# Two pairs projected before the first attention step, and constant products on TensorE, in a gated attention block

## The chip, the cores and the metric

The kernel runs on one NeuronCore of one Trainium2 chip. The metric is the time of one execution in device microseconds. Five engines work side by side, each through its own instructions in their order: TensorE (PE, with its weight loads shown as PEld), VectorE (DVE), ScalarE (ACT), GpSimd (POOL), and SyncE (SP), which here only issues DMAs. Semaphores let one engine wait for another.

## What is computed

One block of a gated cross-attention network, for 4 batches of 512 tokens, width 512. The tokens are normalized twice and rounded to fp8 with a scale for each input. From them come the queries, keys and values of a self-attention (8 groups, 2 heads each, depth 128) and the queries of a cross-attention whose keys and values come from a second sequence. Queries and keys are normalized over their depth. Then a projection and a feed-forward part with ternary weights follow.

```python
ln_out = _ln(hidden_states, ln_w, ln_b)
q = _fp8_linear_pertensor(ln_out, wq, wq_scale, q_in_scale).reshape(b, s, g, hpg, d)
q = _ln(q, qln_w, qln_b)
k = _fp8_linear_pertensor(ln_out, wk, wk_scale, k_in_scale).reshape(b, s, g, d)
k = _ln(k, kln_w, kln_b)
v = _fp8_linear_pertensor(ln_out, wv, wv_scale, v_in_scale).reshape(b, s, g, d)
core = _gqa(q, k, v).reshape(b, s, nh * d)
...
cat = jnp.concatenate([core, xout], axis=-1)
catq = _div_clamp_fp8(cat, proj_smooth)
return jnp.einsum('bsi,oi->bso', catq, wproj) * (proj_in_scale * proj_w_scale)
```

## The kernel before

A *block* is one group of one batch: its queries, keys and values. It is made in two *pairs* (`Pair`, L503), each of two tiles of 128 tokens, so pair k belongs to block k // 2. The order of the blocks is a string in `PLAN` ("ord", two digits for group and batch): the first are group 0, 1 and 2 of batch 0, then groups 1, 0, 2 and 3 of batch 1. Pairs 0 and 1 need the weights of group 0, pairs 2 and 3 those of group 1, pairs 4 and 5 those of group 2, and pair 6 is the first that needs batch 1.

A tile of a pair passes through these steps. `mm` (L519) is 24 products of PE into a PSUM tile of its own (ps_p, one buffer for each half). `sq` (L544) squares queries and keys on ACT (jk), `vals` copies the values (vv), `var` (L554) makes the factors (DVE and POOL, ss). `out` (L571) scales the queries on ACT (z) and then the keys on DVE (y, yj, z), which frees the PSUM tile. When both tiles are out, `split` (L588) writes high and low parts (hl, on ACT and POOL), and `turn` transposes them by DMA into qk.

A *unit* (`Unit`, L604) is one head of one block. For each half of its tokens: `scores` (PE, 8 products into ps_s), `top` (their maxima, mx, DVE), `top_turn` (two transposes, mt, PE), `shift` (nm, DVE) and a DMA of nm into qk, `shift_mm` (4 products that subtract the maximum), `exps` (pt, ACT), `pv` (po, PE, 16 products as the trace counts them) and `evac` and `quant` (r and ob, DVE).

`step(s, k)` (L826) is one unit s with one pair k, in two halves. In each half the scores of the new half unit come first, then the tile that was projected two halves ago is put out, the last one gets its squares, the older half units go on, and `q.mm((h,))` projects a tile of pair k. So a projection waits until the tile two halves back has left its buffer. With s = -1 a step has no new unit, only a pair. The loop at L1173 runs the steps; `extra` says before which of them a step without a unit is put. Before the loop, the head (from L939 on) prepares batch 0, the weights of groups 0 and 1, and projects pairs 0, 1 and 2 by hand.

Work for later pairs lies in `behind`: the rest of batch 1, the weights of group 2 and 3 (`weights_2`, `weights_3`), batches 2 and 3. Each weight chunk (four a group) has a mean and shift (ms), scalings of three 128-column parts (wf), a high part (ACT) and a low part (DVE, wq). `ws` says which engine scales each part: v is DVE, s is ACT. Each batch chunk has four transposes on PE (ps_t), four scalings on ACT (yb) and three operations on DVE (yb, yb, xa). `beside` (L914) hands out pieces in each half against a budget for DVE and ACT (`bg`, and `bg0` where there is no new unit). `at_hook` (L907) puts a batch chunk's transposes inside a projection. `need` (L931) finishes what a pair needs before it starts. `w2` is how many pieces of group 2's weights the head takes, in two places.

The order on each engine is the order of the program while `Ordered.on[0]` is set, for all engines but SP's loads through `sy`. All recorded operations share one line of the code, so the profile shows L75 for them and the tile names tell them apart.

Of the kernel before, what the change touches and what calls it, by code (L numbers as in the profile page):

```python
# [9 lines left out]
F32 = mybir.dt.float32  # L10
# [9 lines left out]
B, S, H = 4, 512, 512  # L20
# [29 lines left out]
    "gain": [66, 69, 74, 77, 82, 85, 90, 93, 98, 101],  # L50
    "ch": [104, 105, 106, *range(108, 116), *range(117, 125)],
    "wp16": 68,
    "extra": {2: 1, 6: 1},
    "none": [],
    "bs": "ssss",
    "w2": [0, 5],
    "ws": "vvs",
    "bg": [1.5, 2.7],
    "bg0": [3.0, 3.0],
}  # L60

# [22 lines left out]
def flamingo_kernel(  # L84
# [18 lines left out]
    cfg = PLAN  # L103
    v, sc, pe, gp, so = [Ordered(tc, e) for e in (nc.vector, nc.scalar, nc.tensor, nc.gpsimd, nc.sync)]
# [11 lines left out]
    ident = const.tile([128, 128], F32, name="ident")  # L116
    make_identity(nc, ident)
    ones = const.tile([128, 128], F32, name="ones")
# [16 lines left out]
    pp_o = keep.enter_context(tc.tile_pool(name="pp_o", bufs=1, space=PSUM))  # L135
# [105 lines left out]
    def consts_out(load_rsr):  # L241
        v.reciprocal(rsm, smo)

        v.tensor_scalar(
            rsm[:, 0:16], rsm[:, 0:16], cs[:, 2:3], 2.0**-8, ALU.mult, ALU.mult
        )
        v.tensor_scalar(
            rsm[:, 16:32], rsm[:, 16:32], 2.0**-8 / KVX_SCALE, None, ALU.mult
        )

        rt = pp_o.tile([128, S], F32, name="rt", tag="po", bufs=1)
        pe.transpose(rt[0:NCH, 0:128], rsm, ident)
        rr = const.tile([NCH, 128], F32, name="rr")
        v.tensor_copy(rr, rt[0:NCH, 0:128])
        so.dma_start(out=rsm_d, in_=rr)
        for i in range(2):
            load_rsr(i)
# [25 lines left out]
    with attn as ph:  # L283
# [25 lines left out]
        def load_rsr(i):  # L309

            rsr[i] = cp.tile([128, 8, 128], F32, name="rsr", bufs=2)
            so.dma_start(
                out=rsr[i].rearrange("p c d -> p (c d)"),
                in_=rsm_d[8 * i : 8 * i + 8].rearrange("c (o d) -> o (c d)", o=1).broadcast_to((128, 1024)),
            )
# [615 lines left out]
        def need(k):  # L931

            blk = pair_block(k)
            for item in list(behind):
                if item[0] in ((blk.ty, blk.g), blk.b):
                    while advance(item) is not None:
                        pass

        Ordered.on[0] = True  # L939
        b0, w0 = Batch(0), Weights(0, 0, wf0)  # L940
        first = consts_first()
# [35 lines left out]
        def scale0(ic, on, ts=range(3)):  # L977
            b0.ps = pss[ic]
            b0.scale(ic, on, ts)
# [36 lines left out]
                b0.fp8(ic, 2)  # L1016
        for p in pairs:
            p.mm((0, 1), (NIC - 1,))
        for ic in range(NIC):
            scale0(ic, "s", (3,))  # L1020
            b0.store(ic)
# [58 lines left out]
        ]  # L1080
        b1.factor()
        consts_out(load_rsr)
        w2 = behind[1]
        for _ in range(cfg["w2"][0]):
            advance(w2)
# [80 lines left out]
        def proj2_mm(ps, t, chunks=range(NCH)):  # L1166
            for c in chunks:
                pe.matmul(
                    ps, cats[t][:, c], wp[c // 12][:, c % 12], start=(c == 0), stop=(c == NCH - 1)
                )  # L1170

        now = 3
        for s in range(n_steps):  # L1173
            Ordered.on[0] = s < n_steps - 3
            if s in (36, 68):
                load_rsr(s // 32 + 1)
            for _ in range(cfg["extra"].get(s, 0)):
                step(-1, now)
                now += 1
            if s in cfg["none"]:  # L1180
                step(s, None)
            else:
                step(s, now)
                now += 1
            to_go = n_steps - s
            if to_go == 4:
                early.update({i: pp_p.tile([128, 512], F32, name="ps_p", tag=f"pp{i}") for i in range(2)})
            for i, chunks in cfg["early"].get(str(to_go), ()):
                proj2_mm(early[i], i, range(*chunks))
# [257 lines left out]
```

## Time and profile before

| What | Value |
|---|---|
| median of 3 runs | 1730.95 us (1727.8 to 1731.91) |
| profiled execution | 1728.55 us |
| its span, first to last instruction | 1726.8 us |
| PE busy | 1639.6 us, 95% |
| DVE busy | 1280.2 us, 74% |
| ACT busy | 1075.1 us, 62% |
| POOL busy | 564.3 us, 33% |

The page of the profile has a row for each engine over 40 equal slices of the span, some 43 us each, in which a digit is the busy share in tenths; the row PEclk is the granted clock of PE in tenths of full speed. Other views answer for a stretch of time: what an engine waited for, its instructions in order of time, or busy times by stretches.

In the first slices PE is busy about half of the time or less, from the fourth on nearly always. Up to about 23 us the clock row says full speed, but 12 products there take 1.89 us (at 18.65) and 1.05 us at 23.66.

### The profile page before, as it was taken

How to read it: one execution, taken by the hardware profiler on the slowest of the kernel's cores; microseconds unless marked ns; L12 is line 12 of the kernel's file. 1: busy time of each engine (PE TensorE's matmuls, PEld its weight loads, DVE VectorE, ACT ScalarE, POOL GpSimd, SP SyncE). 2: the span in 40 equal slices, each digit the busy share in tenths (PEclk: the TensorE clock that was granted, in tenths of full speed). 3: DMA queues.
4: the chain of work that ended last, by engine and by line, in shares of the span. 5: the costliest groups of instructions: out<-in, count | busy, mean ns of one | idle time of the engine just before them, and what ended most of it. 6: DMA issues, size and time to landing. Idle time of an engine off the chain costs nothing.

```text
span 1726.8 us, 40358 instructions
## 1 busy us (share of the span) xinstructions
PE 1639.6 (95%) x14662; PEld 1394.2 (81%) x14662; DVE 1280.2 (74%) x3849; ACT 1075.1 (62%) x3270; POOL 564.3 (33%) x740
## 2 busy tenths in 40 slices
PE   4578999999999998999999999999999999999999
PEld 3468899999999997889999999999999976444444
DVE  8677777777777778877777777777666665679786
ACT  7667676666666666666666666666665543457443
POOL 2223334333334336543444443433333320110000
PEclk8789999999999999999999999999999999999999
DMA  5334445444544556545677676764545684974434
GB/s 166 73 76 82 86 78 96 87 85 87 102 89 87 87 110 137 133 77 114 123 117 123 117 123 117 119 118 93 93 105 111 117 184 151 285 244 110 86 78 87
DMA packets 495144, 196.56 MB, mean 114 GB/s; under 512 B 455232, under 2 KB 463456, under 8 KB 493280
## 3 DMA queue, kind: packets, MB, share of 16 engines
q1 hardware_dynamic: 403888, 139.43, 40.7%
q10 hardware_dynamic: 86448, 50.36, 12.1%
q0 software_dynamic: 4608, 4.20, 1.9%
q8 instruction: 114, 1.87, 0.4%
q14 instruction: 86, 0.70, 0.1%
HBM read 88.90 MB, written 27.28 MB: 67 GB/s over the span
## 4 chain that ended last, share of the span: by engine, by line
PE 77%; DVE 5%; ACT 3%; DMA 3%; issue 2%; POOL 1%; SPq 0%; ACTq 0%
PE ps_p L75 25%; PE po L75 21%; PE ps_s L75 16%; PE psj L75 5%; PE psd L75 3%; PE ub L75 3%; PE ga L75 3%; DMA qk<-nm 2%; PE mt L75 1%; DVE mx L75 1%; ACT yb L75 1%; DVE xa L75 1%; ACT xa L75 1%; DVE nm L75 1%; DVE ob L75 1%
## 5 line engine op out<-in xcount | busy, mean ns | idle before, releaser
L75 PE MATMUL ps_p<-wq,xa 128*128 128x256 f16 (+1 forms) x5584 | 554.2, 256 | 26.9 <-ACT jk L75 13.1
L75 DVE TENSOR_REDUCE mx<-ps_s 128x256 f16<-128x1024 f32 x256 | 334.2, 1305 | 304.9 <-PE ps_s L75 304.9
L75 PEld LDWEIGHTS <-xa 128*128 128x128 f16 x5632 | 480.6, 99 | 77.5 <-issue 15.6
L75 ACT ACTIVATE pt<-ps_s 128x1024 f32<-128x1024 f32 x256 | 262.7, 1026 | 427.0 <-PE ps_s L75 394.7
L75 PE MATMUL po<-vv,pt 128*128 128x129 f32 x4096 | 500.8, 276 | 1.7 <-ACT pt L75 1.7
L75 PEld LDWEIGHTS po<-vv,pt 128*128 128x128 f32 x4096 | 479.1, 192 | 5.1 <-ACT pt L75 2.0
L75 POOL TENSOR_TENSOR ss<-ss,mhalf 128x3 f32<-128x3 f32 (+1 forms) x254 | 220.5, 868 | 738.3 <-DVE ss L75 555.4
L75 PE MATMUL ps_s<-qk 128*128 128x256 f16 x3072 | 421.4, 274 | 9.5 <-DMA qk<-nm 4.2
L75 PEld LDWEIGHTS <-qk 128*128 128x128 f16 x3072 | 286.1, 98 | 40.8 <-issue 9.5
L75 POOL TENSOR_TENSOR hl<-z,hl 128x768 f16<-128x768 f32 x126 | 207.7, 1648 | 94.3 <-ACT hl L75 94.3
L75 ACT ACTIVATE jk<-ps_p 128x128 f32<-128x128 f32 x762 | 201.6, 284 | 10.0 <-PE ps_p L75 8.8
L75 ACT ACTIVATION_READ_ACCUMULATOR jk<-ps_p 128x1 f32 x762 | 164.8, 216 | 0.0
L75 DVE SCALAR_TENSOR_TENSOR ob<-po,r,rsr 128x128 bf16<-128x128 f32 x512 | 156.0, 347 | 8.8
L75 ACT ACTIVATE z<-ps_p,ss 128x127 f32<-128x127 f32 x508 | 156.4, 360 | 7.4 <-issue 3.6
L75 ACT CAST hl<-z 128x768 f16<-128x768 f32 x128 | 106.5, 832 | 28.8 <-POOL z L75 28.8
L75 DVE TENSOR_SCALAR ob<-ob 128x512 bf16<-128x512 bf16 (+2 forms) x384 | 112.1, 292 | 8.8
L75 DVE TENSOR_REDUCE nm<-mt 128x2 f16<-128x256 f16 x256 | 107.0, 418 | 2.0 <-PE mt L75 2.0
L75 PEld LDWEIGHTS <-nt 128*128 128x128 bf16 x512 | 50.0, 98 | 63.6 <-issue 4.3
L75 DVE SCALAR_TENSOR_TENSOR y<-ps_p,ss,gk 128x128 f32<-128x128 f32 x254 | 87.0, 342 | 14.8 <-ACT z L75 9.4
L75 PEld LDWEIGHTS <-cat 128*128 128x128 f16 x512 | 50.0, 98 | 59.1 <-DMA cat<-cat_d 0.9
L75 PE MATMUL mt<-ident,mx 128*128 128x128 f16 x512 | 70.8, 220 | 27.9 <-DVE mx L75 27.9
L75 PE MATMUL psj<-wp,cat 128*128 128x512 f16 x448 | 96.9, 379 | 0.0
(144 smaller groups left out, 1591.3 us busy)
## 6 DMA issues: line engine op xcount, KB each, us to landing
cat_d<-ot ACTq DMA_DIRECT2D x128, 128.0 KB, 2.9
wf<-in_dram ACTq DMA_DIRECT2D x52, 256.0 KB, 3.6
cat<-cat_d SPq DMA_DIRECT2D x13, 1024.0 KB, 5.6
wt<-in_dram ACTq DMA_DIRECT2D x48, 256.0 KB, 4.5
wt<-in_dram SPq DMA_DIRECT2D x24, 512.0 KB, 4.0
xt<-in_dram SPq DMA_DIRECT2D x32, 256.0 KB, 4.0
qk<-nm SPq DMA_DIRECT2D x256, 0.5 KB, 2.0
cf<-in_dram SPq DMA_DIRECT2D x16, 256.0 KB, 2.9
```

What stands on the lines that cost most here:

```text
L75: ins = f(*args, **kw)
```

## The change

Three things are changed, all by the plan and by a helper of four lines.

First, `extra` was one step without a unit before step 2 and one before step 6. Now two such steps stand before step 0. So pairs 3 and 4 are projected before the first scores, and step s is run with pair s + 5 from the start.

Second, `keep_busy(n)` makes n products of `ident` and `ones` into a PSUM tile with the tag "rb", which the transposes ps_t and mt also use, and nobody reads it. It is called with 26 after the last products of pairs 0 and 1, with 32 after `consts_out` (the transpose rt), and with 10 between the two steps without a unit.

Third, `w2` goes from 0 and 5 pieces to 1 and 8, `ws` gives the third scaling of each chunk of groups 2 and 3 to DVE, and `bg` changes a little.

```diff
-    "extra": {2: 1, 6: 1},
+    "extra": {0: 2},
     "none": [],
     "bs": "ssss",
-    "w2": [0, 5],
-    "ws": "vvs",
-    "bg": [1.5, 2.7],
+    "w2": [1, 8],
+    "kb": [26, 32, 10],
+    "ws": "vvv",
+    "bg": [1.4, 2.8],
...
+        def keep_busy(n):
+
+            t_ = pp_o.tile([128, S], F32, name="kb", tag="rb", bufs=1)
+            for _ in range(n):
+                pe.matmul(t_[:, 0:128], ident, ones, start=True, stop=True)
+
...
         for p in pairs:
             p.mm((0, 1), (NIC - 1,))
+        keep_busy(cfg["kb"][0])
...
         consts_out(load_rsr)
+        keep_busy(cfg["kb"][1])
...
-            for _ in range(cfg["extra"].get(s, 0)):
+            for i in range(cfg["extra"].get(s, 0)):
                 step(-1, now)
                 now += 1
+                if s == 0 and i == 0:
+                    keep_busy(cfg["kb"][2])
```

## The prediction

> **What bounds the kernel now.** I began with the busy shares by slice, then took two stretches of the span.
>
> ```profile
> span 1726.8 us, 40358 instructions
> PE   4578999999999998999999999999999999999999
> PEclk8789999999999999999999999999999999999999
> 46.70:160.00 113.30, 80.24 (x764) 71.20 (x765) 75.71 (x220) 76.87 (x228) 31.92 (x40) 0.88 0.33 73
> 160.00:1700.00 1540.00, 1515.25 (x13634) 1295.78 (x13632) 1150.98 (x3474) 959.54 (x2950) 521.14 (x673) 1.00 0.57 116
> ```
>
> The first number after a stretch's length is PE's busy time, the first after the brackets its granted clock. After 160 us PE idles 25 us in 1540: PE is the bound, and the change leaves its instructions there as they were. From 46.7 to 160 us PE idles 33 us of 113 at a mean clock of 0.88. The change works here, so I asked what PE waited for from 28 to 160 us, and read PE's order of time (the first: total, times, longest; the second: start, duration, and in brackets PE's idle time before).
>
> ```profile
> PE mt L75 <- DVE mx L75: 16.0, 7, 5.4
> PE ps_p L75 <- ACT jk L75: 11.2, 6, 3.4
> PE ps_s L75 <- DMA qk<-hl: 2.8, 1, 2.8
> ```
>
> ```profile
> 46.82 1.52 PE L75 MATMUL ps_s<-qk 128*128 128x256 f16 x8
> 53.76 0.39 PE L75 MATMUL mt<-ident,mx 128*128 128x128 f16 x2 [5.43 <-DVE mx L75]
> 54.30 3.43 PE L75 MATMUL ps_p<-wq,xa 128*128 128x256 f16 x24 [0.15 <-DVE yj L75]
> ...
> 83.35 1.94 PE L75 MATMUL ps_p<-wq,xa 128*128 128x256 f16 x24 [3.23 <-ACT jk L75]
> 88.68 3.32 PE L75 MATMUL ps_p<-wq,xa 128*128 128x256 f16 x24 [3.39 <-ACT jk L75]
> ...
> 101.64 0.28 PE L75 MATMUL mt<-ident,mx 128*128 128x128 f16 x2 [1.51 <-DVE mx L75]
> ...
> 126.20 1.04 PE L75 MATMUL ps_s<-qk 128*128 128x256 f16 x4 [2.82 <-DMA qk<-hl]
> ...
> 159.82 0.28 PE L75 MATMUL mt<-ident,mx 128*128 128x128 f16 x2
> ```
>
> The same 24 multiplications (one half of a pair) take 1.94 us at full clock and 3.43 or 3.32 at half. The first scores run at 46.8, but their maxima (mx, DVE) come only at 53.7, since DVE is in the weights of group 2. Pair 5, projected without a unit beside it, has its halves at 83.35 and 88.68: 5.3 us for 1.77 of work. The wait on qk<-hl at 126.2 is pair 5, projected at 83 to 92 and needed by step 4: too small a lead.
>
> **The change, part by part.** Milestones: A is mt of step 1, first half, after the rest of batch 1; B is mt of step 6, first half. From B on both programs have the same order on PE but for a few transposes. Before, B is at 159.82.
>
> *The 26 constants.* PE idles from 28.51 to 37.05. An f32 product of this size costs 0.11 us at full clock (po: 16 in 1.95, less 0.17 for the last to end), so 2.9 us, ending near 31.4. Cover: that pause; at half clock 5.7, still covered. Gain: none. What follows pair 2 is rsm on DVE at 46.64, and DVE's own chain (four statistics after the low parts) sets that, not PE. Without the cover they would cost 2.9.
>
> *The 32 constants* start when rt is done, about 47.0; at half clock 0.22 each, until the clock comes on, so they end between 50.5 and 54. What PE does next is pair 3, first half, which needs pair 2 out of PSUM: statistics, ACT z, then DVE y and yj. That chain now has two weight chunks ahead of it instead of one and a half: DVE's third scaling (0.85 for x3 against 0.60 for x2), one more mean (0.55), shift (0.2) and low (0.62), while ACT saves two scalings of 0.48. Following ACT: norms from 48.1 to 50.95, chunk 0 high 51.8, chunk 1 high (after DVE's scaling, 53.4) 54.0, tanh, z 54.7; then y and yj to 55.4. So pair 3 starts at 55.45, 1.15 later than before, and the constants fit under it. Uncovered they would cost 3.5 to 7. Their worth is that pair 3's halves take 1.77 instead of 3.4, about 2 us of what reaches the next chain.
>
> *Pairs 3 and 4 ahead of step 0.* By the same FIFO walk (jk 0.25 a piece, vv 0.29, yb 2.8, hl 0.8, wf swv 0.3, high 0.53, POOL ss 0.85, z 0.62, y with yj 0.6): pair 3's second half starts at 58.55 (z at 57.8); its transposes let yb run from 60.05 to 62.8; chunk 3's high ends at 63.6, z at 64.15, so pair 4 starts at 64.95. Its second half starts at 67.9 if DVE is not held by POOL's hl and at 70.4 if it is; I take 69. *The 10 constants* wait for yb, since they share the bank of the transposes: 62.85 to 63.95, before 64.95. Cover one us; without it 1.1. Doubled, at half clock, they would delay pair 4 by 0.1.
>
> *Step 0.* PE ends pair 4 at 71.2, scores 72.1, mx 74.0, pair 5 at 74.6, second scores 77.3, pair 5's second half about 79.8 to 81.6. Then the rest of batch 1: before, its first transpose was at 91.84 and mt at 101.64, of which 1 us was half clock; here 81.6 + 9.4 gives A at 91.0. Bounds: 89.5 without a hold, 93 with every hold and cold transposes.
>
> *Steps 1 to 5* are ten halves. Before, the eight halves from 101.64 to 149.95 took 6.04 each. The wait of 2.82 on qk<-hl goes, with about 0.8 of half clock behind it: pair 5 is now projected four units ahead. That gives 5.59. Some of what DVE and ACT caught up in that pause comes back, so I take 5.9: ten halves 59, B at 150.0. Bounds: 5.0 a half is PE's own work (scores 0.87, po 1.79, mt 0.11, shift 0.44, projection 1.77), plus 1.35 of transposes; 6.6 is the dearest half before without the wait (101.64 to 108.27). What is removed there, the two extra pair-only steps, is in these sums: their projections ride inside ten halves.
>
> *DMAs.* Nothing is added. On SP the four loads of group 3 now come ahead of the first nm instead of between them; before, nm waited behind three of them (SP busy 6.71 from 54.78). I cost this at nothing, hidden under pairs 3 and 4; if late, it is one landing, 2.0 us. The budgets 1.4 and 2.8 move background work by a half or so; nothing, hidden under PE's 5 us halves.
>
> **Sum.** 150.0 − 159.8 = −9.8 us. The profiled execution took 1728.55 (span 1726.8 and 1.75 around it), so 1718.75 by its own measure; the median of the runs, 1730.95, lies 2.4 above. I give half of that back: 1720.
>
> **A rule against the constants.** The clock fell at about 33.5, 47.2, 67.7, 88.1 and rose at 43.7, 57.4, 74.5, 91.6. These lie on a grid of 3.4 us.
>
> ```profile
> 30.10:33.50 3.40, 0.00 (x0) 0.00 (x0) 3.11 (x15) 2.46 (x14) 1.34 (x2) 1.00 0.01 5
> 43.80:47.20 3.40, 1.42 (x17) 1.17 (x16) 2.85 (x11) 1.04 (x7) 1.01 (x1) 1.00 0.39 73
> 81.30:84.70 3.40, 1.35 (x17) 1.26 (x18) 2.02 (x8) 2.21 (x11) 0.99 (x1) 1.00 0.55 136
> ```
>
> After the first two stretches the clock fell, after the third it stayed. So it goes by about 1.4 us of work in 3.4.
>
> [...]
>
> **Rivals.**
>
> *The constants don't hold the clock*: the grid's phase puts a poor window on the pause before pair 4 or ahead of pair 3. For it: 10 constants are only 1.1 us, under the 1.4. Against: pair 4's second half waits for z, not for PE. Price: one half at 3.4 and the second transposes late, about 3 us; 1723.
>
> *The gain is given back*: PE gets to batch 2's and 3's preparations sooner, and they are not sooner ready. For it: before, 150 to 156 us hold three waits of 1.4 to 1.7 in which ACT caught up, and that pair-only step is gone. Against: from 160 us on, PE idles 1.6%. Price: 6.6 a half instead of 5.9 (7.0) and 1 in A, leaving 2: 1728.
>
> *Slower: DVE held by POOL.* The third scaling is DVE's in all eight chunks, and DVE stands still while POOL's hl runs:
>
> ```profile
> 104.75 1.65 POOL L75 TENSOR_TENSOR hl<-z,hl 128x768 f16<-128x768 f32 x1 [0.61 <-ACT hl L75]
> 104.78 1.63 DVE L75 SCALAR_TENSOR_TENSOR ms<-ms,sw 128x3 f32<-128x3 f32 x1
> ```
>
> If each chunk meets such a hold, 8 x (1.65 + 0.28) = 15.4, all on high, z, y and the next projection: 15.4 − 9.8 = +5.6, 1735 with the same half of 2.4. It decides from six held chunks on. Against it: only pairs 2 to 6 are split in that time, and 1.65 of y's chain passes beside mx, which is not held (163.40, beside hl at 163.20).
>
> [...]
>
> *It doesn't do what it says*: PE's program shows the three groups and both pairs where the text says, so no chance is kept.
>
> **How the numbers follow.** Forecast 0.60, constants 0.17 (faster too), given back 0.15, slower 0.08. About 0.3%, 5.2 us, is what a measurement of this kernel can tell from no change. Faster 0.77, same 0.15, slower 0.08. The forecast's own range: A and the halves at their low ends give 89.5 + 51.4 = 140.9, 18.9 off, which would need every engine ready at once; I go two thirds of the way from 9.8 to it and no further, 1713. Upward to 1728, where the third case lies.
>
> **What would show it.** In the new trace: pair 3's 24 multiplications in about 1.9 us near 55; the constants ending before pair 3 is ready, at about 0.11 to 0.22 each; mt of step 1 near 91 and of step 6 near 150; no wait on qk<-hl; PE's idle time after 160 us still about 25. It is wrong if B lies after 155, if pair 3 or 4 is ready while constants still run, or if DVE shows weight scalings of over 1 us beside POOL.

## The result, and the profile after

The changed kernel takes 1715.99 us (median of 6 runs, 1714.14 to 1718.43) against 1728.9 before (median of 6, 1726.89 to 1731.91): 12.9 us less. The ratio is 0.9925, with a 95% interval of 0.9911 to 0.9938. Of the profiled execution, 1716.38 us, the span is 1714.5, 12.3 below the 1726.8 of before.

The busy shares by slice and the two stretches of the span, in the changed kernel, with the same columns as before:

```profile
span 1714.5 us, 40637 instructions
PE   5789999999999998999999999999999999999999
PEclk9999999999999999999999999999999999999999
46.70:160.00 113.30, 97.58 (x961) 89.98 (x962) 84.12 (x256) 80.52 (x245) 35.38 (x45) 0.94 0.36 79
160.00:1700.00 1540.00, 1516.43 (x13576) 1291.39 (x13575) 1152.55 (x3469) 958.72 (x2929) 516.88 (x668) 1.00 0.57 116
```

From 46.7 to 160 us PE idles 15.7 us where it idled 33, but 12.97 us of its busy time there are the constants, which nobody reads; after 160 us it idles 24, as before (25). So the time came out of the head. What PE waited for from 28 to 160 us (total, times, longest):

```profile
PE mt L76 <- DVE mx L76: 6.0, 4, 2.5
PE ps_p L76 <- ACT jk L76: 3.8, 4, 1.3
...
PE kb L76 <- ACT yb L76: 2.0, 1, 2.0
```

The maxima cost 6.0 in place of 16.0, and the wait on qk<-hl is gone. The projections' 3.8 in place of 11.2 is not a gain by itself, since constants now stand in these pauses: without them (e1, below) the row reads 15.9. New is the wait of the third group of constants on yb. PE in order of time (start, duration, and in brackets PE's idle time before):

```profile
28.34 6.02 PE L76 MATMUL kb<-ones,ident 128*128 128x128 f32 x52
...
46.61 0.40 PE L76 MATMUL rt<-ident,rsm 128*32 128x128 f32 x1 [2.24 <-DVE rsm L76]
46.80 8.84 PE L76 MATMUL kb<-ones,ident 128*128 128x128 f32 x64
55.68 1.93 PE L76 MATMUL ps_p<-wq,xa 128*128 128x256 f16 x24
...
63.09 4.13 PE L76 MATMUL kb<-ones,ident 128*128 128x128 f32 x20 [1.99 <-ACT yb L76]
67.01 1.97 PE L76 MATMUL ps_p<-wq,xa 128*128 128x256 f16 x24
69.78 1.05 PE L76 MATMUL ps_p<-wq,xa 128*128 128x256 f16 x8 [0.80 <-DVE yj L76]
...
91.36 0.39 PE L76 MATMUL mt<-ident,mx 128*128 128x128 f16 x2 [2.54 <-DVE mx L76]
...
147.95 0.28 PE L76 MATMUL mt<-ident,mx 128*128 128x128 f16 x2
```

The last two rows are the prediction's milestones A (step 1) and B (step 6). B was at 159.82, so 11.9 of the span's 12.3 us are in hand there. The constants stand with twice their number: 26 calls are 52 products, so one call is 0.22 us at full clock. Pairs 3 and 4 are projected at full clock (24 products in 1.93 and 1.97 us).

### The profile page after: what moved, and what is told of

It is laid out like the page before. It is cut to its first block, busy times and chain, and to the rows that moved or that the text cites. A ratio compares the mean times of both kernels' runs of the same rounds, so it can differ in the third digit from the quotient of the medians.

```text
span 1714.5 us, 40637 instructions
## 1 busy us (share of the span) xinstructions
PE 1651.2 (96%) x14798; PEld 1408.6 (82%) x14798; DVE 1280.8 (75%) x3857; ACT 1072.4 (63%) x3262; POOL 563.5 (33%) x740
## 3 DMA queue, kind: packets, MB, share of 16 engines
q10 hardware_dynamic: 86448, 50.36, 12.3%
## 4 chain that ended last, share of the span: by engine, by line
PE 81%; DVE 7%; ACT 5%; DMA 3%; issue 3%; POOL 1%; SPq 0%; ACTq 0%; DVEq 0%; POOLq 0%
PE ps_p L76 26%; PE po L76 22%; PE ps_s L76 17%; PE psj L76 5%; PE psd L76 3%; PE ub L76 3%; PE ga L76 3%; ACT yb L76 2%; PE mt L76 1%; DMA qk<-nm 1%; DVE mx L76 1%; POOL ss L76 1%; DMA ot<-ob 1%; DVE xa L76 1%; DVE ob L76 1%
## 5 line engine op out<-in xcount | busy, mean ns | idle before, releaser
L76 DVE SCALAR_TENSOR_TENSOR z<-y,hk 128x128 f32<-128x128 f32 x256 | 90.2, 352 | 0.0
```

The lines of the kernel that those rows point to most:

```text
L76: ins = f(*args, **kw)
```

## The experiments

The theory was that the lead carries the gain: pairs 3 and 4 are projected while DVE is still in the weights, and pair 5 is early enough for step 4. Its rivals were the clock that the constants hold, and the handling of weights and background work (`ws`, `w2`, `bg`). The gains below are against the runs of before on the same chip. Where the clock's changes fall in the one trace of a run moves the head by a microsecond or two: the first mt is at 75.89 in e6, with pair 4's second half at half clock, and at 74.41 in the change.

**The changed kernel without constants** (e1). The three calls make nothing.

```diff
-    "kb": [26, 32, 10],
+    "kb": [0, 0, 0],
```

> The changed kernel without any of the three groups of constant products. If the gain of 12 us is the lead (pairs 3 and 4 ahead), nine or ten of it stay: 1717 to 1719 us, mt of step 1 (A) at 91 to 94 against 91.36, mt of step 6 (B) at 148 to 151. If it is the clock that the constants hold, most of the gain goes: 1724 to 1729, with pairs 3 and 4 at half clock and B after 155.

1717.27 us, ratio 0.9937 (0.992 to 0.9953). A is at 93.93, B at 149.05. PE in order of time in this run:

```profile
55.30 5.28 PE L76 MATMUL ps_p<-wq,xa 128*128 128x256 f16 x32 [8.67 <-ACT jk L76]
...
66.48 3.57 PE L76 MATMUL ps_p<-wq,xa 128*128 128x256 f16 x24 [4.27 <-ACT jk L76]
70.97 1.86 PE L76 MATMUL ps_p<-wq,xa 128*128 128x256 f16 x8 [0.92 <-ACT jk L76]
```

Pair 4's 24 products take 3.57 us, at half clock, yet the end comes only about 2 us later, within the intervals of both. The constants win 2.6 us at A, of which 1.1 is left at B. Most of the gain is not the clock's: from 46.7 to 160 us the granted clock of this run is 0.86, below the 0.88 of before, and B still comes 10.8 us earlier.

**Constants alone** (e2): the kernel before with the first two groups; there is no pause between pair-only steps for the third.

```diff
+        keep_busy(26)
         for ic in range(NIC):
             scale0(ic, "s", (3,))
...
         consts_out(load_rsr)
+        keep_busy(32)
```

> The kernel before with the first two groups of constants (26 and 32) and nothing else. Lead: no gain, since the first scores now wait behind 8.8 us of constants in place of a pause of 5.4 behind them; 1 to 4 us slower than before. Clock: faster than before by 2 us or more, since the clock is up at 54.

1733.12 us, 1.0029 (1.0019 to 1.0038): 5 us slower, more than expected. The first mt moves from 53.76 to 56.41, behind the constants, and the clock of the steps behind does not make up for it: the granted clock from 46.7 to 160 us rises from 0.88 to 0.91, and B comes 3.1 us later, at 162.88. Where the rest of the 5 us goes stays open. The wait on qk<-hl at step 4 is still there, 3.5 us.

**Lead alone** (e3).

```diff
-    "extra": {2: 1, 6: 1},
+    "extra": {0: 2},
```

> The kernel before with both pair-only steps moved ahead of step 0, with no constants and the old handling of the weights. Lead: 5 to 10 us faster than before, and no wait on qk<-hl at step 4. Clock, or the weights: within 3 us of before.

1723.6 us, 0.9974 (0.9965 to 0.9983): a gain of 4, just under the range given. The trace says more: B is at 151.81, 8.0 us early, the wait on qk<-hl is gone, and about half of the gain is lost again between 160 and 280 us, where PE idles 7.6 us against 3.5 before. This stretch before and in this run (its length, then PE's busy time):

```profile
160.00:280.00 120.00, 116.46 (x1247) 109.05 (x1245) 93.76 (x293) 83.76 (x266) 46.66 (x60) 1.00 0.48 88
160.00:280.00 120.00, 112.41 (x1199) 105.25 (x1198) 96.13 (x283) 80.02 (x252) 43.57 (x56) 1.00 0.46 87
```

No run moves only one of the two steps, so what each of them gives stays open.

**The plan alone** (e4): weights and budgets of the change in the kernel before.

```diff
-    "w2": [0, 5],
-    "ws": "vvs",
-    "bg": [1.5, 2.7],
+    "w2": [1, 8],
+    "ws": "vvv",
+    "bg": [1.4, 2.8],
```

> The kernel before with the third scaling on DVE, the pieces of group 2 taken earlier (1 and 8) and the new budgets; no constants, and the extra steps where they were. Lead: 0 to 3 us slower, since the first maxima wait behind more of DVE's weights. If the handling of the weights carries the gain: 5 us or more faster.

1728.79 us, 1.001 (1.0001 to 1.0019): a trifle slower. The first maxima do wait behind more weights, 8.4 us at the longest wait, and the wait on qk<-hl stays (3.0). So neither the constants nor the plan gains without the lead.

**Which group of constants.** Three runs leave out one group each: the third (e5), the first (e6), the second (e7).

```diff
-    "kb": [26, 32, 10],
+    "kb": [26, 32, 0],
...
+    "kb": [0, 32, 10],
...
+    "kb": [26, 0, 10],
```

> The changed kernel without its third group (26, 32, 0). In the trace of the change a constant counts as two products, and the third group took 4.13 us at half clock (63.09 to 67.22) and held pair 4 back by some 1.8 us. If that delay costs, this is 1 to 2 us faster than the change (1714 to 1715) with A near 90; if the clock that the group raises is worth more, 1 to 2 us slower (1717 to 1718), with pair 4's second half and the first scores at half clock and mt of step 0 at 76 to 77.

> The changed kernel without its first group (0, 32, 10). Prediction's reading: the first group is worth nothing, because pair 2 runs at half clock with or without it (fell at 36.7 instead of 33.6) and DVE's chain to rsm sets what follows: 1715 to 1717, rt within 0.3 us of the change. If it is worth something, rt is later by 1 us or more.

> The changed kernel without its second group (26, 0, 10). If the second group carries what constants give: pair 3 at half clock, yb 1 to 2 us later, and A at 93 to 94 as without any; 1717 to 1718. If the third alone carries it: A at 91 to 92 and 1716.

| Left out | us | ratio (95%) | first mt | A | B |
|---|---|---|---|---|---|
| none (the change) | 1715.99 | 0.9925 (0.9911 to 0.9938) | 74.41 | 91.36 | 147.95 |
| third | 1718.7 | 0.9937 (0.9921 to 0.9952) | 76.20 | 93.14 | 148.24 |
| first | 1717.97 | 0.9932 (0.9915 to 0.9949) | 75.89 | 92.98 | 146.67 |
| second | 1719.77 | 0.9944 (0.9929 to 0.996) | 74.67 | 93.14 | 148.45 |

All intervals overlap, so which group pays is not settled. Two things show in the traces. Without the first group, rt starts at 46.61, where it starts in the change (the other runs with that group have it between 46.66 and 47.10), as the prediction said. Without the third group pair 4 starts 1.6 us earlier, at 65.42 and half clock, and its second half ends later: the first mt is 1.8 us later. But the same can come from where the clock falls in the one trace of a run: without the first group the third takes 2.50 us, at full clock, and the clock falls only behind it, so that pair 4's second half, from 69.67, is at half clock (8 products in 1.89, 1.05 in the change) and the first mt 1.5 us later.

**The third group without its wait** (e13): in the other bank it need not wait for yb.

```diff
-            t_ = pp_o.tile([128, S], F32, name="kb", tag="rb", bufs=1)
+            t_ = pp_o.tile([128, S], F32, name="kb", tag=("rb", "po")[n == 10], bufs=1)
```

> The changed kernel with the third group in the bank of po, so that it does not wait for yb: the ten start at 61, not at 63.1, at full clock, and end near 63.2. If their 4.13 us at half clock cost anything: pair 4 at 65.2 instead of 67.0, and 1 to 2 us faster. If pair 4's second half waits for z and yj alone, as it did: 69.8 and mt of step 0 at 74.4 as in the change, within 0.5 us.

PE in order of time in this run:

```profile
61.32 2.45 PE L76 MATMUL kb<-ones,ident 128*128 128x128 f32 x20
65.75 1.93 PE L76 MATMUL ps_p<-wq,xa 128*128 128x256 f16 x24 [1.98 <-ACT jk L76]
70.24 1.03 PE L76 MATMUL ps_p<-wq,xa 128*128 128x256 f16 x8 [2.56 <-ACT jk L76]
...
74.87 0.28 PE L76 MATMUL mt<-ident,mx 128*128 128x128 f16 x2 [1.39 <-DVE mx L76]
```

The ten now take 2.45 us at full clock, with no wait on yb (1.99 in the change), and pair 4 starts 1.26 earlier than in the change, but its second half and the first mt are no sooner (0.46 later, in a run whose pair 3 was 0.38 later). 1716.02 us, 0.9928 (0.9907 to 0.995): the same. The constants' overrun cost nothing that these runs can tell, since pair 4's second half waits for the chain of pair 3.

**Old budgets in the change without constants** (e9).

```diff
-    "kb": [26, 32, 10],
-    "bg": [1.4, 2.8],
+    "kb": [0, 0, 0],
+    "bg": [1.5, 2.7],
```

> No constants, lead and weights as in the change, but the old budgets 1.5 and 2.7. The lead alone had lost 4 us from 160 to 280 us (PE idle there 7.6 us against 3.6 before) and 2.8 by B. If the budgets cause the late loss: idle 7 us in 160 to 280 and 1720 to 1722. If the handling of group 2's weights causes all of it: 1717 to 1718 and 3 to 4 us idle there.

1722.74 us, 0.9965 (0.9952 to 0.9978), against 0.9937 without constants and with the new budgets: the two numbers of `bg` are worth 0.28%, about 4.8 us. The time is just above its range of 1720 to 1722, and the intervals touch; e3 against e10 below, which differ in the budgets alone, give 0.29% with intervals apart. PE idles 7.6 us from 160 to 280 us; in e1 3.1. The waits there name the maxima. DVE and POOL there (start, duration) with the old budgets:

```profile
197.38 1.28 DVE L76 TENSOR_SCALAR t<-mv 128x4 f32<-128x4 f32 x1
...
261.80 0.40 POOL L76 CAST hl<-z 128x254 f16<-128x254 f32 x1
262.27 2.60 DVE L76 TENSOR_SCALAR yb<-yb 128x1536 bf16<-128x1536 bf16 x2
262.81 1.64 POOL L76 TENSOR_TENSOR hl<-z,hl 128x768 f16<-128x768 f32 x1 [0.61 <-ACT hl L76]
264.90 0.56 DVE L76 TENSOR_SCALAR xa<-yb 128x1536 uint16<-128x1536 uint16 x1
265.38 1.28 DVE L76 TENSOR_REDUCE mx<-ps_s 128x256 f16<-128x1024 f32 x1
```

and the same operation in e1, with the new budgets:

```profile
177.72 1.15 DVE L76 TENSOR_SCALAR yb<-yb 128x1536 bf16<-128x1536 bf16 x2
```

Two roundings take 2.60 us in place of 1.15 when POOL's hl runs (1.64 from 262.81), DVE comes 1.45 late to the maxima, and PE's mt behind them waits 1.64, twice in that stretch (at 178.72 and 266.72). The small operation at 197.38 takes 1.28, where e1 has 0.16 (at 204.13), and PE's mt behind it waits 0.87; by my estimate an hl starts beside it at 196.99 (hl starts 1.07 behind the scaling of ob in the two places where POOL was read, at 174.81 and 262.81, and ob is here at 195.92). The three waits make 4.15 us, where PE idles 4.5 more than in e1. Lead alone has the same two rows of 2.60. With the new budgets these pieces fall where POOL is not splitting (in e1 hl starts at 174.46 and takes 1.6, the roundings start at 177.72), and there is no such row from 160 to 280 us.

**Lead and budgets** (e10): weights as before, no constants.

```diff
-    "extra": {2: 1, 6: 1},
+    "extra": {0: 2},
...
-    "bg": [1.5, 2.7],
+    "bg": [1.4, 2.8],
```

> The kernel before with the lead and the budgets 1.4 and 2.8; weights handled as before, no constants. In the trace with the old budgets DVE takes three of batch 2's statistics between two maxima, with the new ones two. If lead and budgets make the gain together: 1717 to 1720 and 3 to 4 us idle from 160 to 280 us. If the weights are needed too: 1721 to 1724 as with the lead alone.

1720.23 us, 0.9945 (0.9929 to 0.996), with 2.9 us idle from 160 to 280 us: lead and budgets make three quarters of the whole gain. The new handling of the weights adds nothing clear of the scatter: 0.9937 in e1 against 0.9945 here, and with the old budgets 0.9965 in e9 against 0.9974 in e3.

**Budgets alone** (e11).

```diff
-    "bg": [1.5, 2.7],
+    "bg": [1.4, 2.8],
```

> The kernel before with the budgets 1.4 and 2.8 and nothing else. If the budgets are worth 4 to 5 us by themselves: 1722 to 1725. If they are worth it only behind the lead, which uses up the slack of DVE between 160 and 280 us: 1727 to 1730, within 2 us of before.

1730.5 us, 1.001 (1.0001 to 1.002): worth nothing without the lead. Before, PE idled only 3.5 us from 160 to 280, so there was little to win there.

**Smaller budgets for the halves without a unit** (e12), in the changed kernel.

```diff
-    "bg0": [3.0, 3.0],
+    "bg0": [0.5, 0.5],
```

> The changed kernel with 0.5 and 0.5 in place of 3.0 and 3.0 as the budgets of halves without a unit. Pair 4's second half waits behind a chunk of group 3 that nobody needs yet. If that chunk is on the path: pair 4's second half 1 to 2 us earlier, and mt of step 0 at 72.5 to 73.5; what batch 1 leaves for its end may cost 1.6 in A. 1714 to 1717.

1718.18 us, 0.9937 (0.992 to 0.9954): not faster, and just above the range given. Pair 4's second half did start earlier, at 68.77, and the first mt is at 72.97, as expected if the chunk of group 3 is on the path. But A is 92.45, and the shifted pieces of batch 2 meet POOL again: a row of 2.60 at 180.87, beside an hl of 1.64 at 181.41, with a wait of 1.64 behind it, and 6.3 us idle from 160 to 280. A second wait of 1.64, at 266.79, has no held row: there two pairs of roundings, of 1.15 each, stand on DVE ahead of the maxima. So where the pieces fall counts without POOL too. B was 146.71, earlier than in the change, and it was given back.

## Why the prediction was right, point by point

The forecast was 9.8 us off the profiled execution; 12.3 came off the span, and the time, 1715.99, lies inside the range. Its main reason held: the lead is what makes the rest possible, and the milestones are where the walk had put them.

| Step | predicted | measured |
|---|---|---|
| pair 3, first half | 55.45 | 55.68 |
| pair 3, second half | 58.55 | 58.74 |
| pair 4, first half | 64.95 | 67.01 |
| pair 4, second half | 69 (67.9 to 70.4) | 69.78 |
| A | 91.0 | 91.36 |
| one half of steps 1 to 5 | 5.9 | 5.66 |
| B | 150.0 | 147.95 |

*The constants' size* was wrong. The row po has 16 products where the program makes 8 calls, and I put its 0.11 us on a call. A call is two products. The cover still sufficed for the first group (34.36 against 36.97), just sufficed for the second (it ended at 55.64; in e6, with rt at the same time, pair 3 was ready at 55.58), and failed for the third, which ran to 67.22 over a pair 4 that was ready near 65.4 (e5). That this cost nothing that can be told, e13 shows. The first group's worth, none at rt, is shown by e6. The pause behind that group was 2.6 us, where the prediction's 31.4 and 37.05 leave 5.7, and the clock fell in it, at 36.4.

*What they are worth* I put at some 2 us for the second group. All three together, measured, are 2.6 us at A and about 2 at the end, inside the scatter.

*The halves of steps 1 to 5* were the term of the sum that was mis-sized: 0.24 us a half, 2.4 in all. The working behind the 5.9 has a slip. From 101.64 to 149.95 there are eight projections but only seven scores and po; from mt to mt the seven halves up to 146.55 took 6.42 each, and 5.90 without the 3.62 us of the wait and its half clock. So the allowance for what comes back, which made 5.9 out of 5.59, made up for the slip by luck. In the change the wait on qk<-hl went, and the waits on the maxima behind it shrank too, to 0.73 us in ten halves from 3.2 in those seven. Four of the ten halves took 4.98 or 4.99, which is PE's own work, and the dearest 8.52 (118.90 to 127.42, with products at half clock, 16 in 1.91 for 1.06, and a wait on jk of 1.28). In e13, where the clock did not fall in them (the same 16 take 1.06), the ten took 5.37 each.

*"The budgets move background work by a half or so; nothing"* is the step that failed. It is a half or so, and that decides whether DVE's roundings meet POOL (2.60 us for 1.15 in e9). With the old budgets the lead won 4 us (e3), and 6 with the new handling of the weights (e9). No run has them with the constants; with the constants' 2 us I estimate 6 to 8, less than the 9.8 of the forecast. That the change has the new ones was luck for the prediction, which gave them no part in it.

*The rival that the constants don't hold the clock* came in part. The clock fell at about 63.7, before pair 4, and was up again by 67.1, behind 3.40 us of PE's work in the 3.4 from 63.80, nearly all of it constants. The stretch ahead of the fall was not idle:

```profile
60.35:63.75 3.40, 1.42 (x19) 1.24 (x17) 0.60 (x3) 3.37 (x6) 0.00 (x0) 0.99 0.24 77
```

with 1.42 us of PE's work in 3.4 (the first number behind the comma; the rest are PEld, DVE, ACT and POOL, the granted clock, the DMA share and GB/s). In the prediction's stretch from 43.80 it was as much, and behind that the clock fell too.

The prediction's "about 1.4 us of work in 3.4" holds over the traces of before and of the change. In each the clock's changes lie on a grid of 3.41 us, and I took the grid's stretches from 25 to 150 us. At full clock, seven of them had at most 1.30 us of PE's work, and behind each of these the clock fell. It fell behind none of the 43 with 1.76 or more. Of the five between, with 1.41 to 1.51, it fell behind four and stayed up behind one; here one of the change (it fell) and that of before (it stayed; this is the prediction's third stretch, set on the grid):

```profile
118.28:121.69 3.41, 1.51 (x14) 1.14 (x15) 1.99 (x9) 3.38 (x13) 0.10 (x1) 1.00 0.00 0
81.35:84.76 3.41, 1.41 (x18) 1.32 (x19) 2.08 (x8) 2.16 (x11) 1.05 (x1) 1.00 0.55 136
```

*The slower rival* named the right mechanism and the wrong place. It put the hold at the weight chunks; in the change there is one, three weight scalings that take 2.20 us beside hl. Of the other seven rows of three, five take 0.85, one 0.93 and one 1.07:

```profile
115.43 2.20 DVE L76 TENSOR_SCALAR wf<-wf,sw,ms 128x128 f32<-128x128 f32 x3
115.90 1.65 POOL L76 TENSOR_TENSOR hl<-z,hl 128x768 f16<-128x768 f32 x1 [0.61 <-ACT hl L76]
```

One held chunk of eight is far from the six that it needed. The held row here has f32 weights (2.20 for 0.85), those of e9 have bf16 (2.60 for 1.15).

*The gain given back later* did not happen in the change (24 us idle after 160 against 25), but it is what lead alone did, by that hold. For it the prediction counted three waits of 1.4 to 1.7 us between 150 and 156 us before; the rows show two, 1.39 and 1.68, and one of 0.75 at 148.01.

*The signs of being wrong.* Two of the three came: pair 4 was ready while constants still ran, and two rows of weight scalings took over 1 us beside POOL. Neither cost what it was meant to warn of. In the range, two thirds of the way from 9.8 to 18.9 gives 1714, not 1713.

## What to carry to other kernels

Where PE waits through a start-up, move work that needs little into it, then look again at where the background pieces fall: a reordering that is right at its own place can lose half its gain one or two hundred microseconds later to a collision of DVE and POOL (lead alone: 8.0 us at B, 4 at the end, with two rows of 2.60 in place of 1.15). Constant products that keep a clock up are worth what the next chain leaves over, here about 2 us of 13 and inside the scatter, and in the kernel before, where the first scores were ready at once, they were a loss of 5 us. Count products in the trace, not calls in the program, before putting a price on them.

## What the runs showed that was not expected

A call of the constants, on two f32 tiles, is two products and two weight loads in the trace (68 calls, 136 of each): 0.11 us a product at full clock (64 in 7.31 in e13) and about 0.21 in the change's third group, most of which ran at half (20 in 4.13). The clock's changes lie on a grid of about 3.4 us (falls at 36.4, 46.6, 63.7, 91.0 and 121.7 in the change; 33.6, 47.2, 67.7 and 88.2 before) whose phase differs between executions: 47 products of pair 2, the same in all of them, begin at 38.33 in the change and last 6.04 us, and in e7, with the same first group, begin at 38.39 and take 4.71 and, after a gap, 0.93. With where the clock falls B moves by a microsecond or two: B is at 147.95 in the change and at 145.94 in e13, where the clock did not fall behind A (the next 24 products take 1.93 us there, 2.90 in the change). And two numbers of a plan, changed by 0.1 each, were worth nothing in one order of the work and about 5 us in another.
